# Placing a block's products and ScalarE's copies ahead of the addition and the gate in an edge-gated graph kernel

## The chip, the cores and the metric

The kernel runs on one core of a Trainium2 chip. Each of its engines takes instructions from a queue of its own, in the order in which the program puts them down: PE (TensorE, matrix products), DVE (VectorE), ACT (ScalarE), POOL (GpSimd) and SP (which here only starts DMA transfers). They meet through semaphores. The metric is the time of one execution on the device in microseconds, the median of several runs.

## The reference

Sixteen graphs share one adjacency matrix of 1024 nodes, in which about 0.8% of the entries and the diagonal are set. For every edge a gate is computed from both ends, and the neighbours' features are summed twice, with the edge's weight alone and with weight times gate.

```python
pre_u = einsum('bud,dk->buk', h, W1[:d])            # h is x: (16, 1024, 256)
pre_v = einsum('bvd,dk->bvk', h, W1[d:])
hidden = relu(pre_u[:, :, None, :] + pre_v[:, None, :, :] + b1)
S   = sigmoid(einsum('buvk,ko->buvo', hidden, W2)[..., 0] + b2[0])
a_t = einsum('buv,bud->bvd', S * adj, h)
m_t = einsum('uv,bud->bvd', adj, h) * h
z   = beta1*h + beta2*(a_t @ Wa + ba) + beta3*(m_t @ Wm + bm)
```

## The kernel before

Only existing edges are worked on. The 16 batches are taken in four groups of four, the target nodes v in eight tiles of 128. A **block** is one group and one tile: 32 blocks. Each block has ten **steps** (T = 10), two windows of 64 targets with five slots of 128 edges each, so there are 320 steps, n = 0 to 319. Below, k is the block and s = n mod 10 the step in it.

What belongs to one step n:

- `fetch(n)` (L518): a gather on POOL's queue brings, for 128 edges, the row of `table` with pre_u and h of four batches into one of eight `fetched` buffers.
- `expand(n)` (L607): two matmuls on PE spread pre_v of the block's targets (tile `X`, high and low part) over the edges, into the PSUM tile `pc`, of which there are two. Expansion n+2 reuses the buffer that addition n has read.
- `add(n)` (L639): DVE adds `pc` to the gathered pre_u.
- `gate(n)` (L647): four DVE instructions, one per batch, apply relu, multiply with W2 and sum; then ACT takes the sigmoid `gt` (L650) and scales four weight tiles `left` by it (L652). Ahead of each of the four DVE instructions, `fill(n)` may place a piece of the edge lists.
- `left_adj(n)` (L617): ACT makes the ungated weights of a step.
- `aggregate(n)` (L664): PE sums the gathered h with the weights `left` into `acc`. It is done in pairs at odd steps: step n has the aggregations of n-3 and n-2 at its head, each followed by a new gather into the buffer that came free. When half a window is complete, `half_end` copies `acc` to `ev` on ACT (L672). At s=1 and s=6 `load_mark` (L550) casts the next window's marks on ACT.

What belongs to a block is spread over its steps by `products(n, k, s)`; from step 10 (ROOM) to step 309:

- `made_rows`: tables for later groups. PE multiplies with W1's upper half (L445, `w_u`), ACT copies the result to `tab` (L461), SP stores it one step later (L465). It also loads `hT` for a coming block on SP (L434) and starts the copy of x to the table on ACT's queue (L439). The last table rows are made at step 222.
- s=0, 2, 8, 9, `turn_over`: PE transposes a finished part of the sums (L682), ACT copies it to `LT` (L685). `LT` has a single buffer; a new block's begins at s=8. After the second half of a window, DVE multiplies a part of `LT` with h (L696) one or two steps later.
- s=1, 3, 4, 6, 7, `halves(k + 1)`: pre_v of the next block. At s=1 and s=3 a bias row (L449) and eight matmuls (L445, `w_v`) on PE, and two ACT copies, `X` (L482) and `low` (L483). DVE subtracts (L484) at s=5. Casts on ACT follow at s=4 (L486), 6 and 7 (L489).
- s=4 to 7, `block_end(k - 1)`: PE multiplies the previous block's sums with Wa and Wm (L713). After s=5 and s=7 ACT copies the result out of PSUM into a part of `LT` (L718). One step later DVE adds beta1*h (L719), and another step later SP stores 256 KB (L721).

PSUM results of products, transposes and rows share two buffers, `misc`. What is due later is put into a list by `after(step, f)` and called by `do(step)`: L719 at steps s=6 and s=8, L696, L484, and the stores. The edge lists of four node tiles (`lists`, a generator) are made between steps 0 and 110: its pieces that say "op" fill the gaps in `gate`, and those after "slot" or "step" (PE matmuls, ACT copies, two small DVE instructions) are placed by `fill(n, False)`.

Order is written out by hand: with `manual_schedule` the program order is each engine's order. Up to step 9 expansion and products of a step stand ahead of its addition; from step 10 on they stand behind the gate. Step n puts down `add(n + 1)`, `gate(n)` and `expand(n + 2)`.

Of the kernel before, what the change touches and what calls it, by code (L numbers as in the profile page):

```python
# [17 lines left out]
def kernel(  # L18
# [70 lines left out]
    def load_rows(src, n, name, engine=nc.scalar, at_=None):  # L89
        t = const.tile([P, n], FP, name=name) if at_ is None else at_  # L90
        engine.dma_start(t, bass.AP(tensor=src.tensor, offset=src.offset, ap=[[0, P], [1, n]]))
        return t

    def load_weights(src, name, engine=nc.scalar):
        t = const.tile([P, DC, D], FP, name=name)
        engine.dma_start(t, src.rearrange("(c p) k -> p c k", p=P))
        return t
# [304 lines left out]
    def after(step, f):  # L402
        due.setdefault(step, []).append(f)
# [91 lines left out]
    def do(step):  # L495
        for f in due.pop(step, ()):
            f()
# [8 lines left out]
    T = TW * NW  # L506
# [3 lines left out]
    def where(n):  # L510
        k, s = divmod(n, T)
        w, j = divmod(s, TW)
        return k, *order[k], w, j
# [34 lines left out]
    def load_mark(q):  # L548
        marks[q] = big.tile([P, E], FR, name="mark")
        nc.scalar.copy(marks[q], whose[:, order[q // NW][1] * NW + q % NW, :])  # L550
# [51 lines left out]
    def expand(n):  # L602
        k, g, vt, w, j = where(n)
        pcs[n] = psc.tile([P, GD], FP, name="pc")
        for h in range(2):
            c = slice(2 * h * D, (2 * h + 2) * D)
            nc.tensor.matmul(pcs[n][:, c], marks[n // TW][:, j * P:(j + 1) * P], cuts[k][:, w, c],  # L607
                             start=True, stop=True)


    def left_adj(n):
        k, g, vt, w, j = where(n)
        i = vt * NW + w
        m = len(QUARTERS[j])
        o = max(2 * j - 1, 0)
        lefts[n] = wk.tile([P, 2, 2 * GB - 1, V], FP, name="left", bufs=5)
        nc.scalar.activation(lefts[n][:, :m, 1::GB, :],  # L617
                             onehot[:, i, o:o + m, :].unsqueeze(2).to_broadcast([P, m, GB // 2, V]),
                             AF.Copy, scale=val[:, i, j:j + 1])
# [3 lines left out]
    def piece_of(r, n):  # L623

        said = next(r[0], None)
        if said is None:
            running.remove(r)
        else:
            r[1:] = said not in ("slot", "step"), n + {"load": 4, "wait": 2, "slot": 1, "step": 1}.get(said, 0)

    def fill(n, gap=True):
        for r in running:
            if r[1] == gap and r[2] <= n:
                piece_of(r, n)
                break

    def add(n):
        t = fetched[at_slot[n]][:, :GD]
        nc.vector.tensor_tensor(t, t, pcs.pop(n), ALU.add)  # L639

    def gate(n):
        m = len(QUARTERS[n % TW])
        t = fetched[at_slot[n]][:, :GD].rearrange("p (b d) -> p b d", b=GB)
        sc = wk.tile([P, GB], FP, name="sc")
        for b in range(GB):
            fill(n)
            nc.vector.scalar_tensor_tensor(t[:, b, :], t[:, b, :], 0.0, w2_b,  # L647
                                           ALU.max, ALU.mult, accum_out=sc[:, b:b + 1])
        gt = wk.tile([P, GB], FP, name="gt")
        nc.scalar.activation(gt, sc, AF.Sigmoid, bias=b2_b)  # L650
        for b in range(GB):
            nc.scalar.activation(lefts[n][:, :m, 2 * b, :], lefts[n][:, :m, 1 + b // 2 * GB, :],  # L652
                                 AF.Copy, scale=gt[:, b:b + 1])
# [75 lines left out]
    def tail_rows(t, v, m, f):  # L729
        g, vt = order[BS - 1]  # L730
        for i in range(P // m):
            b = g * GB + i + (f * P // m if m == W else 0)
            yield hbs[BS - 1][i * m:(i + 1) * m, f, :], t[b, vt * P + v:vt * P + v + m, :]
# [66 lines left out]
    def products(n, k, s):  # L800
        nonlocal end, parts
        made_rows(n)
        if (s == 2 and 0 < k < BS) or n == total:
            turn_over(k - 1, 1, 1, n)
        z = 3 if n < ROOM else 4
        if z <= s < z + 4 and 0 < k < BS:
            if s == z:
                end = block_end(k - 1)
                next(end)
            go(end, n)  # L810
        if ROOM <= n < total - T:
            if s in (8, 9):
                turn_over(k, 0, s - 8, n)
        elif s == 7 and k < BS:
            turn_over(k, 0, 0, n)
        if s == 7 and k == BS - 1 or s == 8 and n < ROOM:
            turn_over(k, 0, 1, n)
        if (s == 0 and 0 < k < BS) or n == total - 1:
            turn_over(k - (s == 0), 1, 0, n)
        if n == total - 2:  # L820
            end = tail(tails[:2], n)
            next(end)
        elif n == total - 1:
            go(end, n)
        elif n >= total:
            end = tail([tails[2 + n - total]], n)
            next(end)
            go(end, n)
            go(end, n)
        later = n >= ROOM  # L830
        if k + 1 < BS and s - later in (0, 2, 3, 5, 6):
            if s == later:
                parts = halves(k + 1)
                next(parts)
            go(parts, n)
# [4 lines left out]
    total = BS * T  # L840
    ROOM, MORE, LISTS = 10, 3, 110
# [9 lines left out]
    def gather_in(n):  # L851
        aggregate(n)
        free.append(at_slot.pop(n))
        refill()
        fetch_val(1 + (n % 3 == 0))
        if (n + 1) % TW in (0, MID + 1):
            half_end(n, 0 if (n + 1) % TW else 1)

    done = 0
    for n in range(total + 2):  # L860
        k, s = divmod(n, T)
        if n < total - 3:
            last_in = n - 1 if n % 2 or n < ROOM else done
        else:
            last_in = n
        while done < min(last_in, total):
            gather_in(done)
            done += 1
        if n % TW == 1 and n // TW + 1 < total // TW:
            load_mark(n // TW + 1)  # L870
        if n < ROOM:
            if n + 2 < total:
                expand(n + 2)
            products(n, k, s)
        if n + 1 < total:
            add(n + 1)
        if n < total:
            gate(n)
            if n + 1 < total:
                left_adj(n + 1)  # L880
        do(n)
        if n >= ROOM and n + 2 < total:
            expand(n + 2)
        if n == 1:
            w_a = load_weights(Wa, "w_a", nc.sync)
            w_m = load_weights(Wm, "w_m", nc.sync)
            bias = load_rows(bm, D, "bias", nc.sync, spare[:, 1])
            ba_b = load_rows(ba, D, "ba_b", nc.sync, spare[:, 2])
            be1 = load_rows(beta1, 1, "be1", nc.sync)
            be2 = load_rows(beta2, 1, "be2", nc.sync)  # L890
            be3 = load_rows(beta3, 1, "be3", nc.sync)
            after(10, scale_late)
        if s in (5, 7) and k < BS - 1:
            h = s // 7
            hb = big.tile([P, 2, D], FP, name="h_blk", bufs=4)
            hbs.setdefault(k, []).append(hb)
            g, vt = order[k]
            nc.sync.dma_start(hb.rearrange("p b d -> p (b d)"),
                              table[g][vt * P:(vt + 1) * P, GD + 2 * h * D:GD + (2 * h + 2) * D])
        if n == total - 6:  # L900
            hbs[BS - 1] = hT_free.pop(0).rearrange("p b c n -> p b (c n)")
            for v, m, f in tails:
                for h, o in tail_rows(x, v, m, f):
                    nc.sync.dma_start(h, o)
        for i in advance.get(n, ()):
            next(made[i], None)
        if n in start_list:
            running.append([made[start_list[n]], True, n])
            piece_of(running[-1], n)
        fill(n, False)  # L910
        if n >= ROOM:
            products(n, k, s)
        if n == LISTS:
            assert not running and all(next(x, None) is None for x in made)
            lists_done()
            more = main.enter_context(tc.tile_pool(name="more", bufs=1))
            hT_free.extend(hT_places(more, MORE, NH))
        if n == 120:
            nc.gpsimd.partition_all_reduce(longest, rest, P, bass_isa.ReduceOp.max)
            after(n + 12, count_rest)  # L920
# [115 lines left out]
```

## Time and profile before

| | |
|---|---|
| median of three runs | 1101.68 us (1098.24 to 1102.35) |
| profiled execution | 1101.12 us |
| its span, first to last instruction | 1099.3 us |
| busy: PE, DVE, ACT, POOL | 1022.2, 1025.4, 872.5, 464.3 us |
| DMA engines | busy nearly all the span, 359 GB/s in the mean |
| granted TensorE clock, mean | 0.975 |

A row of the profile names the line and engine, the operation, the tile written and the tile read, partitions x elements, how many instructions there are, busy time and mean duration, and the idle time of that engine just before them with what ended it. PE stands for matmuls and PEld for loading their weights, which overlap. In a timeline the first number is the start and the second the duration in microseconds; a wait is in square brackets with what ended it. A list of waits gives the total, the number of times and the longest. A DVE row's duration can be a little longer than its distance to the next, since their ends overlap. The additions of L639 come once a step, in order, so their start times give the length of each block.

### The profile page before, as it was taken

How to read it: one execution, taken by the hardware profiler on the slowest of the kernel's cores; microseconds unless marked ns; L12 is line 12 of the kernel's file. 1: busy time of each engine (PE TensorE's matmuls, PEld its weight loads, DVE VectorE, ACT ScalarE, POOL GpSimd, SP SyncE). 2: the span in 40 equal slices, each digit the busy share in tenths (PEclk: the TensorE clock that was granted, in tenths of full speed). 3: DMA queues.
4: the chain of work that ended last, by engine and by line, in shares of the span. 5: the costliest groups of instructions: out<-in, count | busy, mean ns of one | idle time of the engine just before them, and what ended most of it. 6: DMA issues, size and time to landing. Idle time of an engine off the chain costs nothing.

```text
span 1099.3 us, 23917 instructions
## 1 busy us (share of the span) xinstructions
PE 1022.2 (93%) x7645; PEld 726.5 (66%) x7645; DVE 1025.4 (93%) x3487; ACT 872.5 (79%) x2616; POOL 464.3 (42%) x453
## 2 busy tenths in 40 slices
PE   7777889999899999999999999999999999999986
PEld 6654556776667666676777677767766666666653
DVE  8788888898999999999999999999999999999994
ACT  3347667787778888888988889888889888888873
POOL 2746575445347433563334343433343333333330
PEclk9988989999899999999999999999999999999999
DMA  9999799999999999999999999999999999999991
GB/s 285 331 391 311 295 327 303 356 394 382 384 343 344 391 410 381 384 378 396 408 382 400 406 400 398 386 398 388 353 362 383 372 350 357 359 372 363 354 335 42
DMA packets 149030, 394.54 MB, mean 359 GB/s; under 512 B 18224, under 2 KB 96048, under 8 KB 112688
## 3 DMA queue, kind: packets, MB, share of 16 engines
q0 software_dynamic: 50240, 300.11, 69.6%
q1 hardware_dynamic: 85360, 79.71, 22.9%
q10 hardware_dynamic: 13296, 13.11, 3.6%
q8 instruction: 62, 1.02, 0.3%
q14 instruction: 72, 0.59, 0.1%
HBM read 396.93 MB, written 50.33 MB: 407 GB/s over the span
## 4 chain that ended last, share of the span: by engine, by line
PE 39%; DVE 32%; issue 10%; ACT 9%; DMA 6%; POOL 2%; another core or an unknown queue 0%; SPq 0%; POOLq 0%; DVEq 0%; ACTq 0%
DVE fetched L647 15%; DVE fetched L639 12%; PE acc L664 10%; PE misc L713 10%; PE misc L445 7%; PE pc L607 7%; ACT left L652 3%; PE misc L682 2%; DMA hT<-in_xT_dram 2%; DMA hT<-in_x_dram 2%; PE misc L449 1%; DMA fetched<-table,uidx 1%; DVE low L484 1%; DVE h_blk L719 1%; DVE LT L696 1%
## 5 line engine op out<-in xcount | busy, mean ns | idle before, releaser
L518 POOL DMA_INDIRECT fetched<-table,uidx x320 | 345.5, 1080 | 540.9 <-PE acc L664 384.1
L647 DVE SCALAR_TENSOR_TENSOR fetched<-fetched,w_b 128x256 f32<-128x256 f32 x1280 | 476.5, 418 | 0.0
L639 DVE TENSOR_TENSOR fetched<-fetched,pc 128x1024 f32<-128x1024 f32 x320 | 387.9, 1212 | 38.1 <-PE pc L607 23.1
L652 ACT ACTIVATE left<-left,gt 128x32 f32<-128x32 f32 (+1 forms) x1280 | 299.5, 304 | 10.4
L664 PE MATMUL acc<-fetched,left 128*32 128x256 f32 x4096 | 271.7, 390 | 5.9 <-ACT left L652 4.6
L607 PE MATMUL pc<-X,mark 128*128 128x512 f32 x640 | 245.9, 466 | 12.1 <-DVE fetched L639 12.0
L664 PEld LDWEIGHTS acc<-fetched,left 128*32 128x32 f32 x4096 | 123.7, 111 | 113.1 <-issue 38.8
L650 ACT ACTIVATE gt<-sc,b_b 128x4 f32<-128x4 f32 x320 | 95.5, 298 | 94.8 <-DVE fetched L647 84.4
L607 PEld LDWEIGHTS pc<-X,mark 128*128 128x128 f32 x640 | 106.3, 191 | 91.8 <-issue 48.9
L713 PE MATMUL misc<-w_a,LT 128*128 128x256 f32 x496 | 118.7, 383 | 0.0
L713 PE MATMUL misc<-w_m,LT 128*128 128x256 f32 x496 | 117.2, 379 | 0.0
L445 PE MATMUL misc<-w_v,hT 128*128 128x256 f32 x448 | 108.1, 385 | 1.0 <-DMA hT<-in_xT_dram 1.0
L682 PE MATMUL misc<-ident,ev 128*128 128x128 f32 x512 | 81.3, 282 | 27.0 <-ACT low L483 9.3
L713 PEld LDWEIGHTS misc<-w_a,LT 128*128 128x128 f32 x496 | 94.7, 191 | 15.7 <-issue 0.4
L713 PEld LDWEIGHTS misc<-w_m,LT 128*128 128x128 f32 x496 | 93.9, 189 | 15.2
L617 ACT ACTIVATE left<-onehot,val 128x64 f32<-128x64 bf16 (+1 forms) x320 | 102.9, 322 | 0.0
L385 POOL DMA_INDIRECT val<-in_adjT_dram,vidx x80 | 87.6, 1095 | 33.2 <-issue 18.9
L647 DVE DVE_READ_ACCUMULATOR fetched<-fetched,w_b 128x1 f32 x1280 | 100.4, 78 | 0.0
L682 PEld LDWEIGHTS misc<-ident,ev 128*128 128x128 f32 x512 | 61.2, 143 | 55.1 <-ACT low L483 14.7
L445 PEld LDWEIGHTS misc<-w_v,hT 128*128 128x128 f32 x448 | 86.6, 194 | 16.0 <-DMA hT<-in_xT_dram 1.9
L672 ACT COPY ev<-acc 128x512 f32<-128x512 f32 x128 | 74.7, 584 | 15.4 <-PE acc L664 6.8
L685 ACT COPY LT<-misc 128x512 f32<-128x512 f32 x128 | 73.1, 572 | 5.6 <-PE misc L682 2.9
(178 smaller groups left out, 974.6 us busy)
## 6 DMA issues: line engine op xcount, KB each, us to landing
h_blk<-table SPq DMA_DIRECT2D x62, 256.0 KB
out_dram<-h_blk SPq DMA_DIRECT2D x62, 256.0 KB
hT<-in_xT_dram SPq DMA_DIRECT2D x28, 512.0 KB
table<-in_x_dram ACTq DMA_DIRECT2D x24, 512.0 KB
table<-tab SPq DMA_DIRECT2D x48, 256.0 KB
fetched<-table,uidx POOLq DMA_INDIRECT x320
table<-in_x_dram SPq DMA_DIRECT2D x8, 512.0 KB
table<-fetched SPq DMA_DIRECT2D x8, 512.0 KB
```

The lines of the kernel that those rows point to most:

```text
L385: nc.gpsimd.indirect_dma_start(out=val[:, i, j:j + 1], out_offset=None, in_=adj_flat, in_offset=bass.IndirectOffsetOnAxis(ap=vidx[:, i, j: ...
L445: nc.tensor.matmul(p[:, bb * D:(bb + 1) * D], hT[:, 2 * h + bb, i, :], wt[:, i, :], start=(i == 0 and not begun), stop=(i == DC - 1), skip ...
L518: nc.gpsimd.indirect_dma_start(out=fetched[at_slot[n]], out_offset=None, in_=table[g], in_offset=bass.IndirectOffsetOnAxis(ap=uidx[:, vt * ...
L607: nc.tensor.matmul(pcs[n][:, c], marks[n // TW][:, j * P:(j + 1) * P], cuts[k][:, w, c], start=True, stop=True)
L617: nc.scalar.activation(lefts[n][:, :m, 1::GB, :], onehot[:, i, o:o + m, :].unsqueeze(2).to_broadcast([P, m, GB // 2, V]), AF.Copy, scale=v ...
L639: nc.vector.tensor_tensor(t, t, pcs.pop(n), ALU.add)
L647: nc.vector.scalar_tensor_tensor(t[:, b, :], t[:, b, :], 0.0, w2_b, ALU.max, ALU.mult, accum_out=sc[:, b:b + 1])
L650: nc.scalar.activation(gt, sc, AF.Sigmoid, bias=b2_b)
L652: nc.scalar.activation(lefts[n][:, :m, 2 * b, :], lefts[n][:, :m, 1 + b // 2 * GB, :], AF.Copy, scale=gt[:, b:b + 1])
L664: nc.tensor.matmul(accs[h][b * 2 * V:(b + 1) * 2 * V, r, :], left[:, i, 2 * b - b % 2:2 * b - b % 2 + 2].rearrange("p k v -> p (k v)"), f[ ...
L682: nc.tensor.transpose(pt[:, r, :, c, :], ev[:, r, c * P:(c + 1) * P], ident)
L713: nc.tensor.matmul(pz[:, bb * D:(bb + 1) * D], LTs[k][:, 2 * h + bb, i if bb else 1 - i, c, :], wt[:, c, :], start=False, stop=(i == 0 and ...
```

## The change

From step 10 to step 309, expansion n+2, the list pieces of `fill(n, False)` and `products(n, k, s)` stand ahead of `add(n + 1)` and `gate(n)`. Since `turn_over` at s=8 takes the single `LT` buffer anew, and the L719 of that step still reads the old one, `do(n)` is called ahead of the products at s=8; so that L719 stands ahead of the addition and the gate on DVE. The steps 0 to 9 and the last block (from step 310) keep their order.

```diff
@@ for n in range(total + 2) @@
-        if n < ROOM:
-            if n + 2 < total:
-                expand(n + 2)
+        if n < total - T:
+            expand(n + 2)
+            if n >= ROOM:
+                fill(n, False)
+                if s == 8:
+                    do(n)
             products(n, k, s)
         if n + 1 < total:
             add(n + 1)
@@ after gate(n) and left_adj(n + 1) @@
         do(n)
-        if n >= ROOM and n + 2 < total:
+        if n >= total - T and n + 2 < total:
             expand(n + 2)
@@ at the end of a step @@
-        fill(n, False)
-        if n >= ROOM:
+        if n < ROOM:
+            fill(n, False)
+        if n >= total - T:
             products(n, k, s)
```

## The prediction

> **What bounds the kernel now.** I read the engine totals first, then a table by stages, then the waits of each stage, then the timeline of single blocks. Step n's addition is the n-th instruction of L639, so the table can be cut at whole blocks of ten steps: 101.40 is step 10, 323.40 step 70, 453.10 step 110, 819.50 step 230, 1050.40 step 310. Below, s is the step within its block.
>
> ```profile
> PE 1022.2 (93%) x7645; PEld 726.5 (66%) x7645; DVE 1025.4 (93%) x3487; ACT 872.5 (79%) x2616; POOL 464.3 (42%) x453
> ```
> ```profile
> core 0: us, PE busy (x) PEld busy (x) DVE busy (x) ACT busy (x) POOL busy (x), PEclk, DMA share, GB/s
> 101.40:323.40 222.00, 204.50 (x1456) 145.59 (x1455) 202.15 (x710) 166.67 (x498) 116.98 (x115) 0.94 0.95 346
> 323.40:453.10 129.70, 123.33 (x955) 88.47 (x958) 125.82 (x432) 108.15 (x328) 59.35 (x56) 1.00 1.01 378
> 453.10:819.50 366.40, 358.20 (x2791) 258.87 (x2784) 351.06 (x1151) 322.04 (x971) 145.88 (x131) 1.00 1.02 389
> 819.50:1050.40 230.90, 222.52 (x1755) 152.70 (x1748) 230.90 (x762) 205.95 (x633) 82.57 (x81) 1.00 0.96 363
> ```
> Four regimes. Blocks 1-6 (37.0 us each): nobody is full, DVE is idle 19.9 us and PE 17.5. Blocks 7-10 (32.4 us): list pieces fill DVE. Blocks 11-22 (30.53 us), which still make table rows on PE: PE is 98% busy. Blocks 23-30 (28.86 us), rows done: DVE is busy every microsecond and PE waits. Waits of PE in 101.4 to 323.4, then of PE in 483 to 789, then of DVE in 300 to 1040 (total, times, longest):
> ```profile
> PE misc L445 <- ACT low L483: 3.8, 2, 3.1
> PE misc L682 <- ACT LT L685: 3.5, 3, 1.5
> PE misc L682 <- issue: 3.3, 1, 3.3
> ```
> ```profile
> PE misc L682 <- ACT low L483: 5.1, 8, 0.7
> ```
> ```profile
> DVE fetched L639 <- PE pc L607: 14.5, 20, 1.2
> ```
> So before step 230 PE waits for ScalarE's copies and DVE for PE's expansion. A late block, in order of time:
> ```profile
> 929.80 1.89 PE L713 MATMUL misc<-w_m,LT 128*128 128x256 f32 x8
> 931.77 1.21 DVE L639 TENSOR_TENSOR fetched<-fetched,pc 128x1024 f32<-128x1024 f32 x1
> 931.88 0.30 ACT L650 ACTIVATE gt<-sc,b_b 128x4 f32<-128x4 f32 x1
> 933.31 0.56 ACT L718 COPY LT<-misc 128x512 f32<-128x512 f32 x1
> 934.28 0.74 DVE L719 SCALAR_TENSOR_TENSOR h_blk<-h_blk,be,LT 128x512 f32<-128x512 f32 x1
> ...
> 942.41 0.73 ACT L550 CAST mark<-whose 128x640 fp32r<-128x640 uint8 x1
> 943.04 0.30 ACT L650 ACTIVATE gt<-sc,b_b 128x4 f32<-128x4 f32 x1
> 943.36 0.96 ACT L652 ACTIVATE left<-left,gt 128x32 f32<-128x32 f32 x4
> 943.74 1.21 PEld L664 LDWEIGHTS acc<-fetched,left 128*32 128x32 f32 x16 [0.43 <-ACT left L652]
> 945.36 0.73 PE L607 MATMUL pc<-X,mark 128*128 128x512 f32 x2
> ```
> The first five rows are step 7's last product, the addition for step 9, step 7's gate, ScalarE's copy of that product, and the L719 add of step 8 that reads the copy. The others are s=1's gate, whose weights PE already waits for.
>
> **The change, part by part.** Nothing is added or removed; 300 steps are reordered. On PE nothing moves: aggregation, expansion, list matmuls, products follow each other as before. On POOL nothing passes anything (the gathers already stood first). On SP, a block load (L434) now stands ahead of its own step's store (L721 or L465) instead of behind; mostly they fall in different steps; taken as zero, at worst some early start. On ACT, each block's copies, with the ACT-queued table copy (0.56 us, L439), pass the gate of their own step; DVE's list pieces after a slot pass one addition and gate. The moves that matter are two: **copies ahead of the gate** on ScalarE, and, at s=8, **L719 ahead of the addition** on DVE.
>
> Blocks 11-22. At s=2 PE's L682 waited 0.66 us (timeline, 586.76) because the low copies of s=1 stood behind that step's gate. The same instruction comes again at 617.25, 30.49 us later; less its wait (0.58 to 0.66) PE's own path is 29.85 us a block. But later gates cost something back: with L719 at t=0, ACT runs the last cast (to 0.97), gate 7 (2.25), two copies, gate 8 (DVE done at 3.20; to 4.65), the ev copy (5.34); PE wants ev at 5.22, and gate 9's weights, ready at 6.98, at 6.87. About 0.35 us of stall, so 30.20 against 30.53: 0.33 x 12 = **-4.0 us** (0 to -8, all of the wait gone).
> Here a rule of the Trainium skill (Perfetto Trace Analysis, Identifying the Most-Contended Engine) disagrees: it holds matmul busy time a poor measure of headroom and would have weight loading instead. That is 258.87 of 366.40, 71%: PE would have room, DVE's 351.06/12 = 29.26 us would be the floor, and the gain up to 1.27 x 12 = 15 us. But the timeline has PE's instructions of heavy steps back to back and DVE waiting 1.10 us for L607 at 609.14; I take the row.
>
> Blocks 23-30. DVE is full, so no copy can help; but L719 now stops DVE until step 7's product is copied. The loop, in pieces measured around 905-946: L719 0.67, then three steps (addition and gate, 934.95 to 937.46, 2.51 each) to the end of s=0's gate: 8.20. To ScalarE 0.11; from that gate's start (940.09) to the end of s=1's weights (944.32) 4.23, less the LT copy that now stands before (0.46), plus X and low that now stand between (0.95): 4.72. Last weight to PE's next L607 (945.36) 1.04. From that L607 to the end of step 7's last product (916.50 to 931.69) 15.19. Copy and two hand-overs 0.04+0.56+0.07. Sum **29.93** against 28.86: 1.07 x 8 = **+8.6 us**. Before, the same loop lacks one addition and gate and the two copies (about 27), and lies hidden under DVE's 28.86. In blocks 11-22 the same loop gives 29.96, below PE's 30.20, so it costs nothing there; if PE's cover went, it would take over.
>
> Blocks 7-10. Blocks 7 and 8 are like 11-22: -1.0. In 9 and 10 (33.9 us) DVE's lists are longer than the loop: -0.5. Together **-1.5** (0 to -3.8, DVE's whole idle time).
>
> Blocks 1-6. The PE waits that end in an ACT copy are 3.8+3.5 and, from the same view, 1.5 (L682 on tab), 1.4 (L341 on LT) and 0.9 (L682 on left), 11.1 in all, and the 3.3 marked issue is one too: L682 started at 157.92, the low copy ended at 157.86. Bounds: 14.4 gained, or a few us lost to L719 (2 us of DVE stall in a block where it comes early, against DVE's idle 3.3 per block). DVE also waits 6.3 us for what the view calls remote (most likely gathers), which stays. I take a little under half, **-6**.
> The granted clock here is 0.94, and PE ran at half speed after the 3.34 us wait at 157. The skill's TensorE: Matmul & The Clock Gate (Part 1: The HAM clock gate) says one idle window, about 3.4 us, halves the clock. By it, shorter waits would return part of 0.06 x 222 = 13 us, and the late stalls, 1.07 us a block more than now, would halve nothing. By the row I can't tell which waits did it (0.86 came in 287-323 too), so the sum has none of it and the low end has some.
>
> Step 310 on is unchanged, as are steps 0-9. **Sum**: -4.0 + 8.6 - 1.5 - 6 = -2.9 us on the profiled execution's 1101.12 (span 1099.3 and 1.8 around it): 1098.2. The median of the runs, 1101.68, stands 0.6 above that execution; between the two, **1098.5**.
>
> **Rivals.**
> L719 doesn't stop DVE: PE, relieved at s=2 and s=8, runs far enough ahead that the copy is there when DVE comes. For it: from the end of the addition put down at s=6, DVE needs 4.6 us to L719 (two gates of 1.38, an L719 of 0.67, an addition of 1.13), while the expansion which that addition frees, the product and its copy take 0.56+1.89+0.6 = 3.1. Against: step 7's product ends (931.69) when DVE finishes gate 7 (931.8) already now. Then the late blocks stay: -4.0-1.5-6 = -11.5, 1090.
> L719 stops DVE in blocks 11-22 too (slower): gate 7 ends on DVE at 602.26, the copy can't be ready before 604.6. That 2.35 us exceeds DVE's idle 1.3 per block; unless DVE runs later than now against PE, a block takes 29.26+2.35 = 31.6, +1.1 x 12 = 13, with +8.6 late and -6 early: +15.6, 1117. It decides from a stall of 1.3 us a block on, where DVE's idle time is used up.
> Nothing net: the early waits only change their name (ACT's copies now wait for PE's products, and the gate behind them), the early blocks give some 3 us instead of 6, and the gains just pay the late loss: 1101.5.
>
> **How the numbers follow.** Chances: forecast 0.45 (own range 1093 to 1102), no stop 0.28, stop everywhere 0.12, nothing net 0.15. Half a per cent (5.5 us, below 1096.2 or above 1107.2) is about what a measurement of this kernel tells from no change. Faster: 0.14 of the forecast and 0.28, 0.42. Same: 0.30 and 0.13, 0.43. Slower: 0.12 and 0.03 of tails, 0.15. The range 1087 to 1107 holds the first, second and fourth case and their unknown early blocks; it leaves out the slow rival (0.12) and a low tail (some 0.06) in which the early clock recovers as well.
>
> **What would show it.** A new DVE wait at L719 on ACT L718, about 1 us a block after step 230, blocks there of 29.9, PE waiting for left L652 at s=3. No L682 wait on low in 483-789, blocks of 30.2. Fewer PE waits on ACT before 323. It is wrong if late blocks keep 28.9, or blocks 11-22 exceed 30.6.

## The result, and the profile after

Timed beside the kernel before, in 22 runs each, the changed kernel has a median of 1099.8 us (1094.26 to 1108.01), the kernel before 1102.41 us. The ratio is **0.9983**, with a 95% interval of 0.9965 to 1.0001: 1.9 us by the ratio, and the interval reaches no change. A ratio is taken over the runs of one occasion, without those that are over 1.5% above the fastest of their kernel, and so is not the quotient of the two medians. The profiled execution took 1097.05 us (span 1095.2) against 1101.12 (span 1099.3).

On a later occasion, beside the last three variants below, the same changed kernel took 1111.31 us (1106.73 to 1118.63, 16 runs) against 1105.25 us before (47 runs): **1.0049**, 1.0024 to 1.0074. So by the ratios one program was once 1.9 us ahead of the kernel before and once 5.4 us behind. The experiments look for where these 7 us lie.

The engine totals of the profile after:

```profile
PE 1029.3 (94%) x7645; PEld 735.7 (67%) x7645; DVE 1020.8 (93%) x3487; ACT 862.0 (79%) x2616; POOL 465.5 (42%) x453
```

The table by stages, cut at the same additions as before (steps 10 to 70, 70 to 110, 110 to 230, 230 to 310), first in the profile after, then in the changed kernel's profile from the later occasion:

```profile
core 0: us, PE busy (x) PEld busy (x) DVE busy (x) ACT busy (x) POOL busy (x), PEclk, DMA share, GB/s
102.56:313.87 211.31, 200.11 (x1497) 145.41 (x1495) 201.10 (x712) 164.59 (x497) 119.74 (x117) 0.99 1.01 367
313.87:444.80 130.93, 126.90 (x948) 90.97 (x946) 125.50 (x433) 107.44 (x327) 57.80 (x57) 0.97 1.00 378
444.80:807.12 362.32, 359.79 (x2772) 261.32 (x2770) 347.55 (x1146) 315.79 (x971) 146.08 (x131) 1.00 1.02 393
807.12:1046.47 239.35, 228.91 (x1731) 156.90 (x1728) 231.41 (x763) 205.17 (x632) 81.81 (x80) 1.00 0.92 345
```
```profile
103.37:320.62 217.25, 205.99 (x1499) 148.01 (x1498) 201.75 (x712) 164.57 (x497) 116.21 (x116) 0.98 0.98 356
320.62:450.48 129.86, 124.57 (x948) 89.50 (x946) 125.54 (x433) 107.56 (x327) 59.11 (x56) 1.00 1.01 385
450.48:820.10 369.62, 364.68 (x2772) 261.94 (x2770) 347.69 (x1146) 316.56 (x971) 140.78 (x131) 1.00 1.01 385
820.10:1059.33 239.23, 228.77 (x1731) 156.52 (x1728) 231.31 (x761) 205.15 (x632) 84.71 (x80) 1.00 0.93 347
```

The second number of a row is the stage's length. Against before (222.00, 129.70, 366.40, 230.90) the profile after has -10.7, +1.2, -4.1 and +8.5, in all -5.1; the start up to step 0 and the steps 0 to 9, which the change doesn't touch, add -1.8 and +3.0, and the end -0.1, which comes to the span's 4.1 but for rounding. The later profile has -4.8, +0.2, +3.2, +8.3. The last stage is the same in both. The first differs, and so does the third: 362.3 or 369.6 for the same blocks 11-22.

The late stage first. Two lists of waits of the profile after from step 230 to step 310, the rows of DVE and PE taken out of them, and then one block in order of time, by the chain that ended last between 900 and 960:

```profile
PE acc L664 <- ACT left L652: 9.3, 16, 0.7
...
DVE h_blk L719 <- ACT LT L718: 7.9, 8, 1.0
```
```profile
906.14 1.69 PE acc L664 x15
...
921.22 1.74 PE misc L713 x8
922.99 0.60 ACT LT L718
923.64 0.36 issue
924.27 1.21 DVE fetched L639
925.49 1.08 DVE fetched L647 x7
926.87 1.13 DVE fetched L639
928.26 0.82 DVE fetched L647 x6
929.38 1.14 DVE fetched L639
930.78 0.82 DVE fetched L647 x6
932.26 0.90 ACT left L652 x4
933.40 0.47 ACT ev L672
933.87 0.63 ACT mark L550
934.49 0.48 ACT X L482
934.98 0.48 ACT low L483
935.69 0.33 ACT left L652
936.06 1.69 PE acc L664 x15
```

DVE waits once a block at L719, 0.99 us each, for the copy of step 7's last product. From there the chain goes through three additions and gates, then through ScalarE (weights, ev, marks, `X` and `low`, and only then the last weights) to PE, which comes to its next last product. The same row stands at 906.14, so a round takes 29.92 us, and the late blocks take 29.89 to 29.93 against 28.86.

Over the whole profile, PE's idle time just before the matmuls of L664 rose from 5.9 to 19.4 us, and DVE's before L639 fell from 38.1 to 11.5. DVE waits less for PE's expansion, and PE waits for ScalarE's weights instead:

```profile
L639 DVE TENSOR_TENSOR fetched<-fetched,pc 128x1024 f32<-128x1024 f32 x320 | 387.9, 1212 | 11.5 <-PE pc L607 5.0
L664 PE MATMUL acc<-fetched,left 128*32 128x256 f32 x4096 | 287.3, 389 | 19.4 <-ACT left L652 19.3
```

### The profile page after: what moved, and what is told of

The parts are those of the page before. It is cut to its first block, busy times and chain, and to the rows that moved or that the text cites. A ratio compares the mean times of both kernels' runs of the same rounds, so it can differ in the third digit from the quotient of the medians.

```text
span 1095.2 us, 24089 instructions
## 1 busy us (share of the span) xinstructions
PE 1029.3 (94%) x7645; PEld 735.7 (67%) x7645; DVE 1020.8 (93%) x3487; ACT 862.0 (79%) x2616; POOL 465.5 (42%) x453
## 4 chain that ended last, share of the span: by engine, by line
PE 58%; DVE 17%; ACT 12%; DMA 8%; issue 4%; POOL 0%; DVEq 0%; SPq 0%; ACTq 0%; POOLq 0%
PE misc L713 16%; PE acc L664 14%; PE misc L445 13%; PE pc L607 9%; DVE fetched L647 7%; DVE fetched L639 6%; ACT left L652 3%; PE misc L682 2%; DMA fetched<-table,uidx 2%; PE misc L449 2%; DMA hT<-in_xT_dram 2%; ACT X L489 1%; ACT LT L718 1%; DMA table<-tab 1%; DMA key<-in_adjT_dram 1%
## 5 line engine op out<-in xcount | busy, mean ns | idle before, releaser
L639 DVE TENSOR_TENSOR fetched<-fetched,pc 128x1024 f32<-128x1024 f32 x320 | 387.9, 1212 | 11.5 <-PE pc L607 5.0
L652 ACT ACTIVATE left<-left,gt 128x32 f32<-128x32 f32 (+1 forms) x1280 | 299.5, 305 | 10.4
L664 PE MATMUL acc<-fetched,left 128*32 128x256 f32 x4096 | 287.3, 389 | 19.4 <-ACT left L652 19.3
L607 PE MATMUL pc<-X,mark 128*128 128x512 f32 x640 | 244.8, 464 | 16.2 <-DVE fetched L639 14.6
L664 PEld LDWEIGHTS acc<-fetched,left 128*32 128x32 f32 x4096 | 133.9, 110 | 131.9 <-ACT left L652 42.3
L607 PEld LDWEIGHTS pc<-X,mark 128*128 128x128 f32 x640 | 106.0, 191 | 96.4 <-issue 35.4
L385 POOL DMA_INDIRECT val<-in_adjT_dram,vidx x80 | 89.8, 1122 | 33.6 <-issue 16.1
L482 ACT CAST X<-misc 128x512 fp32r<-128x512 f32 x64 | 37.3, 583 | 59.8 <-PE misc L445 59.7
L685 ACT COPY LT<-misc 128x512 f32<-128x512 f32 x128 | 73.1, 572 | 7.0 <-PE misc L682 5.9
## 6 DMA issues: line engine op xcount, KB each, us to landing
hT<-in_xT_dram SPq DMA_DIRECT2D x28, 512.0 KB, 20.5
```

Of the source, the lines that this page charges most:

```text
L385: nc.gpsimd.indirect_dma_start(out=val[:, i, j:j + 1], out_offset=None, in_=adj_flat, in_offset=bass.IndirectOffsetOnAxis(ap=vidx[:, i, j: ...
L664: nc.tensor.matmul(accs[h][b * 2 * V:(b + 1) * 2 * V, r, :], left[:, i, 2 * b - b % 2:2 * b - b % 2 + 2].rearrange("p k v -> p (k v)"), f[ ...
```

## The experiments

The theory: L719 ahead of the addition closes a loop DVE, ScalarE, PE, DVE, which is longer than DVE's own work in the late blocks, and it costs all that the copies ahead of the gate gain elsewhere. The rivals: the copies `X` and `low`, now ahead of the gate on ScalarE, do it alone; or the stages' differences are noise of single executions and the parts sum to nothing. The first four variants ran beside one another, then the next four, then the last four beside one another. Ratios are to the kernel before, from the same occasion.

**The change without its late part.**

```diff
-        if n < total - T:
+        new = n < ROOM or n < 230
+        if new:
```

> The new order only in steps 10 to 229, the old one from step 230 on. Theory (the loop through L719 costs 1.07 us in each of the eight late blocks, nothing else there differs): late blocks back at 28.86 us with DVE full, so 8.5 us under the changed kernel (1099.8), about 1091, and faster than the kernel before by some 11 us (1.0%). Rival (the late loss is paid back in the last block or by an earlier start): late blocks 28.9, but the time stays within 3 us of the changed kernel.

Measured: 1099.04 us, ratio 0.9956 (0.9933 to 0.9979). The late stage is back at 230.91 us, blocks of 28.86, and DVE has no idle time in it. The late loss is the late part's own. The whole time missed its 1091 and stayed within the rival's 3 us of the changed kernel's 1099.8, which comes from another occasion. In this profile blocks 11-22 took 366.36 us, 4 more than in the profile after (blocks 16 to 18 took 30.9 us and block 11 took 32.1), and steps 10 to 70 took 218.41, 7 more.

**The late part alone.**

```diff
+        new = n < ROOM or 230 <= n < total - T
```

> The new order only in steps 230 to 309. Theory: late blocks 29.9 us, all before them as before: +8.5 us on the kernel before, about 1111, ratio 1.008. Rival (the loss is local to the profile, or a shift between stages): within 3 us of before.

Measured: 1115.04 us, ratio 1.0088 (1.0045 to 1.0132), late stage 239.41 us, blocks of 29.9. This is as expected: the loop costs 8.5 us, and the rest of the program has no part in it.

**The L719 add back behind the gate.** The result of the second block-end product is copied to a tile of its own (`sums`, free by then), so that nothing forces L719 ahead at s=8; the rest is the change.

```diff
+                if h == 1 and step >= 120:
+                    z = sums.rearrange("p i w q v -> p (i w q v)").rearrange("p (b d) -> p b d", b=2)
                 nc.scalar.copy(z, pz.rearrange("p (b d) -> p b d", b=2))
...
-                if s == 8:
+                if s == 8 and not n >= 120:
                     do(n)
```

> The change, but from step 120 on the second copy of block_end (s=7) goes to a place of its own (the constant sums, not used any more by then) instead of LT, so that the L719 of s=8 can stay behind the gate. ScalarE's order and PE's are those of the change. Theory (L719 ahead of the addition closes the loop, the X and low copies only lengthen it): without L719 at the head the loop has one addition and gate less, 29.93-2.51 = 27.4, under DVE's 28.86: late blocks 28.9, DVE full, and blocks 12-22 at PE's own 29.9 to 30.1; in all about 10 us under the changed kernel, 1090. Rival (the copies ahead of the gate make the weights of s=1 late by themselves): late blocks stay near 29.9, time within 3 us of the changed kernel's.

Measured: 1098.31 us, ratio 0.9942 (0.9923 to 0.9962). From block 24 on, blocks take 28.98 to 29.03 us with DVE idle for 0.06 us or less, so the loop is gone with the place of L719 alone. In blocks 13-22 the period stays at 29.8 to 30.3 us, and PE is idle 0.07 us in such a block: there PE's own work is the limit, not this loop. The whole time missed its 1090; by the ratios this version is some 4.5 us ahead of the change in its first comparison.

**The copies back behind the gate, L719 left ahead**, from step 230 on.

```diff
+            if not ((230 <= n < total - T) and s == 1):
                 go(parts, n)
...
+        if (230 <= n < total - T) and s == 1 and k + 1 < BS:
+            go(parts, n)
         do(n)
```

> The change, but from step 230 on the first part of halves (s=1: a bias row, eight matmuls, the X and low copies) stands behind the gate again; PE's order is the same, only the two copies move on ScalarE. L719 still stands ahead of the addition. Theory (one loop, its pieces add): 29.93-0.95 = 28.98 us a late block, 7.6 us less than the changed kernel in all, about 1092, with a DVE wait at L719 of only 0.1 us. Rival (L719's stop alone is enough): late blocks 29.5 or more.

Measured: 1101.52 us, ratio 0.9974 (0.9951 to 0.9998); late blocks of 28.99 to 29.02 us, which is the sum of the prediction (29.93) less the two copies (0.95). DVE still waits 0.07 to 0.12 us at L719 in each of them, as expected, so the loop is still what ends last, by a tenth. Taking either half out of the change shortens the loop to about DVE's own work: in the new order the loss needs both L719 ahead of the addition and the two copies ahead of the gate. The whole time missed its 1092; blocks 11-22 took 367.02 us in this profile.

**L719 ahead, and nothing else.** The kernel before, with `do(n)` ahead of the addition at s=8.

```diff
+        if ROOM <= n < total - T and s == 8:
+            do(n)
         if n + 1 < total:
             add(n + 1)
```

> The kernel before with one move: at s=8 of steps 10 to 309 the L719 add (do(8)) stands ahead of the addition; ScalarE's copies stay behind the gate. Theory (the copy that L719 reads then follows gate 7 on ScalarE, so DVE stands from the end of its gate 7 for 1.14+0.31+0.56+0.14, about 2.1 us): late blocks 31.0, blocks 11 to 22 30.5 to 31.4, in all 20 to 35 us over the kernel before. Rival (the stop is short, since PE and ScalarE are ahead): late blocks under 29.9, as in the change.

Measured, in one run: 1147.8 us, 46 more than the median before (1101.68) and more than the 20 to 35 expected. Late blocks take 31.0 us, as forecast; blocks 12-22 take 31.65, over the 31.4 forecast, and blocks 7-10 together 135.95. Of the waits between 500 and 800, the row of DVE at L719:

```profile
DVE h_blk L719 <- ACT LT L718: 20.8, 9, 2.4
```

With the product behind the gate, as before, L719 stops DVE by 2.3 us a block there and by 2.06 in the late blocks. The change moves the products forward too, and by that shortens this wait to 1.23 and 0.99 us.

**The early steps alone** (10 to 69), and **blocks 11-22 alone** (steps 110 to 229).

```diff
+        new = n < ROOM or 10 <= n < 70
```

> The new order in steps 10 to 69 alone. Theory (ScalarE's copies no longer hold PE up there, and PE's clock is halved less often): these six blocks 217 to 220 us against 222 to 225, granted clock there 0.98 against 0.94; in all 6 us under the kernel before, ratio 0.9945. Rival (the stage varies from run to run by as much, and PE's waits there are for gathers and lists): within 2 us.

Measured: 1101.98 us, ratio 0.9973 (0.9949 to 0.9998); in steps 10 to 70 216.35 us at a granted clock of 1.00, as good as expected; the whole time has about half the expected gain.

```diff
+        new = n < ROOM or 110 <= n < 230
```

> The new order in steps 110 to 229 alone, L719 ahead of the addition. Theory (PE's path per block is 30.15 us once L682 no longer waits for low): blocks 12 to 22 at 30.15, block 11 about 1 us longer for L719's stop, 3.5 us under the kernel before in all, ratio 0.997; clock before step 110 as in the kernel before. Rival (L719's stop is the bound there too): blocks of 30.5 or more, ratio 1.000 or more.

Measured: 1103.83 us, ratio 0.9995 (0.9970 to 1.0019). The stage took 368.39 us, 2 more than before, where the profile after has 4.1 less, and neither account fits all of it. Its blocks are of two kinds, though all run the same order: 12, 13, 14, 16 and 17 took 30.9 to 31.2 us, 15 and 18 to 22 took 30.13 to 30.19.

**The parts put together**: new order in steps 10 to 99 and 110 to 229, the former one in the late blocks, and the place of its own for the second copy from step 110 on.

```diff
+        new = n < ROOM or n < 100 or 110 <= n < 230
...
+                if h == 1 and step >= 110:
```

> The new order where it paid (steps 10 to 99 and 110 to 229), the old one elsewhere; from step 110 on the second copy of block_end goes to its own place, so that L719 stays behind the gate. Theory (gains and losses of the stages add): steps 10-70 -6 us, 70-110 -1.5, 110-230 -5, 230-310 none: 12 us under the kernel before, ratio 0.989. Rival (what is gained early is lost in the wait for the lists to end, about step 110): ratio 0.994 or more.

Measured: 1097.81 us, ratio 0.9935 (0.9909 to 0.9961), nearer to the rival's 0.994 than to the 0.989 expected. Steps 110 to 230 took 364.12 us, and steps 70 to 110 took 131.94, more than the 129.70 of before.

**Four versions on one occasion.** Since the change and its variants had been timed on different occasions, the change, the version without the late part, the one with the place of its own, and a cut of the parts that leaves blocks 7-10 as they were ran side by side.

> The change as it is, again, beside the next three on one chip. Theory: the late blocks' loop of 29.9 us a block gives back most of what the early steps and the blocks of the rows gain, so it ends 2 to 3 us ahead of before, ratio 0.998. Rival (the gap that the first comparison left between it and its parts came from the chip, not from the kernels): ratio 0.995 or less, as the version without the late part.

> The change without its late part (the steps from 230 on in their former order), on the same chip as the change. Theory: the loop alone parts them, 8 blocks by 1.04 us, so this is 8.4 us faster than the change: ratio to before 0.990 to 0.991. Rival: the blocks of the rows at 30.9 us instead of 30.15 come more often without the late part, three blocks or more in most executions, and take 2 to 5 us of it: ratio 0.993 to 0.996.

> The change with the second block-end copy in a place of its own from step 120 on, so that the step function's product L719 stays behind the gate. Theory: late blocks of 29.0 us as in the former order, blocks of the rows at 30.15 without the slower kind, so 7 to 9 us faster than the change: ratio 0.990 to 0.992. Rival, as for the one above: 0.994 to 0.996.

```diff
-        new = n < ROOM or n < 100 or 110 <= n < 230
+        new = n < ROOM or n < 70 or 110 <= n < 230
```

> New order in steps 10 to 69 and 110 to 229, the former one in blocks 7 to 10 and in the late blocks, and the second block-end copy in a place of its own from step 110 on. Theory: it keeps the early steps' 4.4 us and the rows' 0.35 us a block (4 us), and saves the 1 us that blocks 7 to 10 lost: 1 us under the version that had the new order in blocks 7 to 9 too, ratio 0.991 to 0.993. Rival (blocks 7 to 10 cost nothing, what they lose comes from the clock): the same as that one, 0.9935.

| | median, us | ratio to before | steps 10-70 | 70-110 | 110-230 | 230-310 |
|---|---|---|---|---|---|---|
| before (profile shown ahead) | 1105.25 | 1 | 222.0 | 129.7 | 366.4 | 230.9 |
| the change | 1111.31 | 1.0049 (1.0024 to 1.0074) | 217.3 | 129.9 | 369.6 | 239.2 |
| without its late part | 1104.61 | 0.9981 (0.9953 to 1.0009) | 220.0 | 131.4 | 368.9 | 230.9 |
| place of its own | 1100.11 | 0.9955 (0.9929 to 0.9981) | 217.3 | 131.4 | 363.4 | 233.6 |
| cut of the parts | 1096.28 | 0.9930 (0.9895 to 0.9965) | 216.7 | 128.4 | 363.6 | 231.7 |

The change missed both of its expectations; it was slower than before. Without the late part it is 6.7 us faster than with it (0.68 points of ratio), somewhat less than the 8.3 by which the late stage differs, and its ratio, 0.9981, missed both of its expectations too. Its rival, blocks of 30.9 us that come more often without the late part, falls: the change has six of them here, the version without the late part five. The version with a place of its own came out in its rival's range, but not by the rival's cause, since no block of 13-22 took over 30.5 us in its profile; blocks 23, 24 and 26 took 29.4 to 29.7 us there, the other late ones 29.0 to 29.1. The cut of the parts has the lowest ratio of the study, 0.7% ahead of before, but from seven runs: its interval holds the ratios of the parts put together and of the place of its own, and can't tell its theory (0.991 to 0.993) from its rival (0.9935).

**What the slower blocks are.** In blocks 12-22 of the six profiles that have the new order there with L719 ahead, 24 of 66 blocks took 30.9 to 31.2 us, and almost all others 30.13 to 30.25 (three of block 12 took 30.4 to 30.8). Every one of the 24, and none of the others, has an idle time of 0.6 to 0.9 us on ScalarE ahead of the L685 copy of s=9. The same copy with its neighbours on ScalarE, in block 14 of the profile after (30.14 us) and in block 14 of the later profile (30.95 us):

```profile
537.43 0.56 ACT L672 COPY ev<-acc 128x512 f32<-128x512 f32 x1
537.89 0.57 ACT L685 COPY LT<-misc 128x512 f32<-128x512 f32 x1
538.39 0.30 ACT L650 ACTIVATE gt<-sc,b_b 128x4 f32<-128x4 f32 x1
538.63 1.67 PE L664 MATMUL acc<-fetched,left 128*32 128x256 f32 x24
538.72 0.90 ACT L652 ACTIVATE left<-left,gt 128x16 f32<-128x16 f32 x4
```
```profile
546.17 0.56 ACT L672 COPY ev<-acc 128x512 f32<-128x512 f32 x1
...
547.37 1.07 PE L664 MATMUL acc<-fetched,left 128*32 128x256 f32 x16
547.47 0.58 ACT L685 COPY LT<-misc 128x512 f32<-128x512 f32 x1 [0.74 <-PE misc L682]
547.95 0.30 ACT L650 ACTIVATE gt<-sc,b_b 128x4 f32<-128x4 f32 x1
548.28 0.90 ACT L652 ACTIVATE left<-left,gt 128x16 f32<-128x16 f32 x4
548.64 1.21 PE L664 MATMUL acc<-fetched,left 128*32 128x256 f32 x8 [0.20 <-ACT left L652]
```

In the first the copy follows ev at once, and the sigmoid and weights of step 9 come in time for PE. In the second the copy starts 0.82 us later in its block, the weights with it, and PE, with 24 matmuls to do, stops after 16 and then goes on at the pace at which weights arrive (8 matmuls in 1.21 us). PE has 0.07 us to spare in a block of 30.14, so this one is 0.8 us longer. Six such blocks are 4.9 us, and blocks 11 and 12, longer by 1.8 and 0.5, bring it to 7.2 of the 7.3 by which this stage differs between the two profiles of one kernel.

Three profiles with the former order in this stage have 366.4, 366.6 and 367.4 us, mean 366.8. In the new order with L719 ahead they are 362.3, 366.4, 367.0, 368.4, 368.9 and 369.6, mean 367.1: no gain. With L719 back behind the gate the stage takes 361.6, 363.4, 363.6 and 364.1, mean 363.2: a gain of 3.6 us. There only 3 of 44 blocks have the wait of the copy, against 24 of 66.

What makes the copy late is settled by half. The traces also record when each semaphore changes, and the copy waits for the one that PE raises at the end of a group of matmuls. In block 14 of the profile after PE raises it at 1.77, 2.23 and 2.95 us after the block's first addition, each time within 0.02 us of the recorded end of its group (these transposes, the expansion, the next transposes); the copy starts at 2.13, when ScalarE is done with ev. In block 14 of the later profile the same groups are recorded at the same places, but the three raises come together, at 2.94, 2.98 and 3.04, and the copy starts at 2.96. So it is in all 24 delayed blocks: the raise comes at 2.85 to 3.11 us, and the copy 0.02 to 0.03 after it. ScalarE starts as soon as it may; what is late is PE's signal, and perhaps the matmuls with it, since the profile's ends of matmuls are modelled.

In blocks 13-21 of the five profiles with delayed blocks, 45 in all, one such signal is always late. In 22 it is that of the transposes; in 22 it is that of the L664 matmuls ahead of them, at 1.36 to 1.44 us instead of 0.70, for which a gather waits but not the copy, and the block takes 30.13 to 30.19 us; in one it is that of the transposes, by less (30.23 us). In the former order the signal of the same transposes is late too, by 0.4 to 0.5 us in 26 of the 27 blocks 13-21, but there the copy stands behind the gate, and ScalarE, busy with the weights until then, is idle 0.03 us at most.

Why PE's signals come late is **not settled**. PE, ScalarE and DVE have the same instructions in the same order in both blocks shown, and which blocks are hit changed from one occasion to the next. The profile after, the one without a late signal there, is also the only one of the fourteen with all its semaphore records; the others lack 7 to 9% of PE's and 18 to 23% of ScalarE's. So the recording itself may have a part in it. No run here tests a cause.

## Why the prediction was right, and where it was not

**The forecast** of 1098.5 us stands 1.3 us under the median of the first comparison, 1099.8, and its range (1087 to 1107) holds that. It does not hold the 1111.31 of the later occasion. That the number came so close is partly luck: of its four terms only the late one, +8.6, came out in every profile that has it; the profile after owes its gain to early blocks that were 4.7 us better than forecast, and over the mean of the profiles the four terms would have made the kernel 6 us slower. The rival of nothing net (1101.5) isn't excluded by the time, since the interval reaches no change, and the early gain of some 4 us is nearer to its 3 than to the 6 forecast.

**The late loop: right.** The sum was 29.93 us a block, and the profile after has 29.92 by the chain and 239.35 - 230.90 = 8.45 us for the stage (8.6 forecast). It was built from seven pieces of the trace of before, and the chain after runs through these same pieces. Without the two copies the sum gave the blocks too, 28.99 to 29.02 against 28.98; without L719 ahead the loop no longer showed, and blocks came down to DVE's own work. The rival without a stop, 1090, falls with the 0.99 us of wait in each block.

**Blocks 11-22: the size right in the first profile, the step incomplete.** The forecast was 30.20 us a block, and it's 30.14 to 30.19 where ScalarE is in time. The sum's term that failed is "about 0.35 us of stall": it counted the copies that now stand ahead of gate 9 as work of fixed length, and asked only whether the weights (ready at 6.98) come much after PE wants them (6.87). One of these copies waits for PE itself, and where PE's signal came late, the block took 0.8 us more, twice what it had gained. The place had been named: gate 9 was the one with no slack. What was not asked is what a wait of the copy would do there. Behind the gate it had cost nothing.

**PE's room in blocks 11-22: rightly read.** By the Trainium skill's page Perfetto Trace Analysis (Identifying the Most-Contended Engine), PE's room is to be read from its weight loads, 71% in this stage (and from MFU, its share of the peak rate, which wasn't worked out here), which made DVE's 29.26 us the floor. The row was taken, and it was right: with L719 back behind the gate DVE is idle 1.2 us a block and the block still takes 30.15, with PE idle 0.07. The wait at 609.14, read in the prediction as one for L607, stands in the view as one for L664; both are PE's.

**L719 in blocks 11-22: right, with little to spare.** The rival that ends slower was put to decide "from a stall of 1.3 us a block on". The stall was 1.23 in the profile after (12.3 us in 10 waits, steps 120 to 220) and 1.77 in the later one. Its 31.6 us a block came true in the variant in which L719 alone moved (31.65): there DVE waits 2.3 us for the copy. In the change, the products that move with it save about a microsecond of that.

**Blocks 7-10: wrong in sign.** Forecast -1.5, measured +1.2 in the profile after. Over the profiles, 128.9 us in the former order (five) and 130.5 in the new (seven), +1.6: blocks 8 and 10 lose 1.2 and 1.7, block 9 gains 1.3, block 7 stays. From step 70 to 120 DVE waits at L719 for 3.7 us in the profile after and 6.5 in the later one, up to 2.9 at a time, and not at all in the profile of before. The failed part is "DVE's lists are longer than the loop": true of their sum, but L719 stands in the middle of them, and what stands behind it can't fill its wait. How much of the 1.6 us this makes isn't shown: block 10 was also long, 36.4 us, in the parts put together, which have the former order there. That blocks 7-10 are better left alone is also what the cut of the parts has, 128.4.

**Blocks 1-6: right in direction.** Forecast -6. The profile after has -10.7, but that is the best of ten; their mean is 217.4 us, and the three of the former order have 222.0, 224.5 and 217.9, mean 221.5. So -4, with a spread between executions as large. PE's half-speed time in this stage, left out of the sum for want of a row, was 27.3 us before and 3.4 after; over all profiles 27.3, 20.5 and 6.8 in the former order against 0 to 10.4 in the new. In the mean that is 12 us less at half speed, which could be worth up to 6 by an estimate from these figures, so the clock can be the whole early gain: the one profile in the former order that had only 6.8 us at half speed took 217.9, half a microsecond over the mean of the new. PE's idle time in the stage did fall, from 17.5 to 21.6 us to 11.2 to 15.8. That the shorter waits spared the clock is argued, not shown. In the late stage the granted clock stayed at 1.00, as forecast.

**The sum.** With the mean stages, -4.1 + 1.6 + 0.3 + 8.4 = +6.2 us, where the later occasion measured 5.4 by the ratio and 6.1 by the medians. With the profile after, -5.1. That the change lies between by how often one copy is late is inferred from one profile of each occasion.

## What to carry to other kernels

A wait that a single buffer forces onto a busy engine is priced by closing the loop through every engine it touches, piece by piece from the trace; where the sum exceeds that engine's own work, it sets the period, and giving the buffer a second place removes it. When a copy that waits for another engine is put ahead of work that a full engine needs next, ask what its lateness does in either place: here it was free behind the gate, and ahead of it a start 0.8 us late made the block 0.8 us longer. And one profile of each kernel isn't enough where the margin is a tenth of a microsecond: compare the stages of several, and time the parts of a change on one occasion.

## What the runs showed that was not expected

Two profiles of one program, with the same order in every queue, differ by 7.3 us in one stage, mostly through a start of one copy that is either at once or about 0.8 us late, with few values between. Once late, it is not late for good: slow and fast blocks alternate (13 to 15, 17, 19 and 20 slow, 16, 18, 21 and 22 fast).

The start of the kernel alone, up to the first addition, took 63.5 to 72.2 us over the profiles, with nothing changed in it; so a difference of a few microseconds between two single executions says nothing about a change in the middle, and the stages must be compared.
